# A linear-attention and FFN kernel on one core: pairs 5 and 6 turned back by a float32 product that takes the mean off, and the last pair scaled in two steps on ScalarE

## The chip, the cores and the metric

The kernel runs on one core of one Trainium2 chip. The metric is the device time of one execution in microseconds (us), the median over several runs. Engine names are those of the profile: PE (TensorE matmul), DVE (VectorE), ACT (ScalarE), POOL (GpSimd), SP (SyncE, which here only issues DMAs).

## The reference, cut to what matters

The input has 16 sequences of 256 tokens with 128 features, in float32. Twelve layers of attention without a softmax come first; then a layer norm, a gated FFN with integer weights, and a second layer norm. Only the end concerns the change:

```python
x = layernorm(x + attn(x))             # no weight, no bias; eps 1e-5
gate, up = x @ wg.T, x @ wu.T          # weights = int / 127, 384 hidden
h = silu(gate) * up
x = layernorm(x + h @ wd.T)            # (x - mean) / sqrt(var + eps), over 128 features
```

## The kernel before

The 16 sequences are worked on as 8 pairs (0 to 7) of 512 tokens each. A planner (`Plan.run`) puts the order of all instructions together when the program is built: every step is an `op` with a cost in ns for each engine that may do it, the values it reads and writes, and a due time (`prio`). The planner always emits, of the steps that could start first, the one that is due first, and gives it to the engine on which it would end first. So a changed cost or a changed list of engines for one step can move others. Each engine then works through its own list in order, and waits for other engines with semaphores.

The function `ffn(p, prio)` emits all of the work of a pair after the attention. In it, with the lines of the profile:

- `mm_r` (L675, L677) makes the tokens' rows of the residual sum in PSUM. `norm(pr, True)` is the first layer norm; its input already has zero mean ("centred").
- `tr_x` (L683) turns the result so that features lie on partitions. L205 or L207 takes a rounded high part `xh` (tile `yhl`), L686 the low part `xl` (tile `thl`), L691 or L693 the whole (tile `kv`).
- For each of three blocks of 128 hidden features: gate and up products (L706 and L707 on high and low part, 128x512 each), a Silu on ACT (L709), its product with up on DVE (L710, tiles `xt` and `qgv`), a rounded copy `hh` (L205 on ACT, L207 on DVE), the rest `hl` (L210, on POOL or DVE), and the down products (L719, L720). The third block of pair 7 goes without the split: L723, a float32 product straight from the tile that L710 wrote.
- L732 (DVE) adds the residual to the down products in PSUM, still with features on partitions. `tr_o` (L736) turns four blocks of 128 tokens back on PE. For pair 7 both are cut in two halves with a PSUM bank each.
- `norm(po, False, po2)` is the last layer norm: `stats` (L618, two instructions on DVE), `var` (L621 `ve`; L623 `nm` = minus the mean), `rstd` on POOL (L634, the power -0.5 of `ve`, and L636, `nb` = `nm` times that power), and the scaling on ACT (L650, four instructions that take `nb` as bias and the power as scale). For pair 7 the first half is scaled on DVE (L648, subtracts the mean and multiplies in one), the second on ACT (L650).
- L743 stores the pair: SP issues the DMA, for the second half of pair 7 ACT does.

A centred norm needs neither L623 nor L636; ACT scales it with the power alone (L646), or DVE does the whole pair in one instruction (L641). `center` is a 128x128 float32 matrix, the identity minus 1/128, built at the start.

Of the kernel before, what the change touches and what calls it, by code (L numbers as in the profile page):

```python
# [13 lines left out]
AF = mybir.ActivationFunctionType  # L14
ALU = mybir.AluOpType
# [6 lines left out]
C = 128  # L22
# [4 lines left out]
NP = B // PB  # L27
# [7 lines left out]
N = PB * T  # L35
K = N // 128
G = 4
NO = NP // G
OB = G * PB
WARM = 30  # L40


# [31 lines left out]
PE, ACT, DVE, POOL, SP = "pe", "act", "dve", "pool", "sp"  # L74
# [92 lines left out]
def mm32(n=C):  # L167
    return max(220, 4 * n / 2.4 + 8)
# [6 lines left out]
def act(n, sbuf=False, pointers=0):  # L175
    return (94 if sbuf else 51) + 93 * pointers + n / 1.2


def dve(n, fast=False):
    return 69 + n / (1.92 if fast else 0.96)  # L180
# [6 lines left out]
def flat(t):  # L187
    return t.rearrange("p a b -> p (a b)")
# [3 lines left out]
def linear_attention_ffn_kernel(ctx: ExitStack, tc: tile.TileContext, x, xt, wall, wq0, bias, wg, wu, wd, out):  # L192
    nc = tc.nc
# [7 lines left out]
    bank = lambda v: banks[v.slot]  # L201
# [10 lines left out]
    def mul(e, dst, a, b):  # L212
        (nc.vector if e == DVE else nc.gpsimd).tensor_tensor(dst, a, b, ALU.mult)  # L213
# [8 lines left out]
    for t in xtoks:  # L222
        nc.vector.memset(t[:, :, C:], 1.0)
    for _ in range(WARM):
        nc.tensor.matmul(banks[7][:, :128], zero, zero, start=True, stop=True)
    tst = new("tst", [B, W])
    nc.gpsimd.memset(tst[:, :, C:], 0.0)
    ident = new("ident", [128])
# [5 lines left out]
    center, centerr = new("center", [128]), new("centerr", [128], F32R)  # L234
# [136 lines left out]
    def offset_products(l, o):  # L371

        raw, pc = wts[l][0], Val("bank")
        c = tst[:, o * OB : (o + 1) * OB, C]

        def mm():
            for s in range(1 if l else 0, 3):
                for g in range(G):
                    cols = slice(32 * g, 32 * g + 32)
                    nc.tensor.matmul(bank(pc)[cols, s * OB : (s + 1) * OB], wraw[raw.slot][:, s * C : (s + 1) * C][:, cols], c, start=True, stop=True)  # L380
        return [raw, *vc[o * G : (o + 1) * G]], pc, mm

    def offsets(l, o, prio, pc):


        bs, ps = slice(o * OB, (o + 1) * OB), slice(o * G, (o + 1) * G)
        c = tst[:, bs, C]
        step = lambda costs, f, reads, writes: plan.op(costs, f, reads, writes, prio)
        src = lambda s: bank(pc)[:, s * OB : (s + 1) * OB]
        step({DVE: 133}, lambda e: nc.vector.tensor_scalar(vb[:, bs], src(2), bcol[:, l, 2:3], None, ALU.add), [pc, vbias], [vvc[o]])  # L390
# [3 lines left out]
        step({DVE: dve(32 * OB)}, lambda e: nc.vector.transpose(flat(vbb[:, bs]), vb[:, bs].unsqueeze(2).to_broadcast([128, OB, 32])), [vvc[o]], [vvb[o]])  # L394
        step({DVE: dve(32 * OB)}, lambda e: mul(e, kvo[:, bs], vbb[:, bs], kb[:, bs].unsqueeze(2).to_broadcast([128, OB, 32])), [vvb[o], vkb[o]], [vkvo[o]])

# [182 lines left out]
    for p in range(NP):  # L579
        t = {f"{n}{j}": new(f"{n}{j}_{p}", [512], F32R) for n in ("hh", "hl") for j in range(NB)}  # L580
# [14 lines left out]
    def ffn(p, prio):  # L595

        x = xts[p]
        t = lambda n: ctxs[p][n]
        bs = slice(p * PB, (p + 1) * PB)
        chunks = lambda a: a.rearrange("p (k c) -> p k c", c=C)  # L600
        v = {n: Val() for n in ("tt", "st", "rs", "x1", "xh", "xl", "sg0", "sg1", "hh0", "hh1", "hl0", "hl1")}

        def op(costs, emit, reads, writes):
            plan.op(costs, emit, reads, writes, prio)

        def norm(src, centred, other=None):


            xs, rows = t("x1"), lambda: bank(src)
            cut = lambda a, k: a[:, k * C : (k + 1) * C]  # L610
            row = lambda k: cut(bank(other if other and k >= K // 2 else src), k)

            def stats(e, ks=range(0, K, 2)):

                for k in ks:
                    b = bank(other if other and k else src)
                    both = b[:, k * C : (k + 2) * C].rearrange("p (k c) -> p c k", c=C)
                    nc.vector.bn_stats(t("st")[:, k : k + 2, :].rearrange("p k s -> p (k s)"), both)  # L618

            def var(e):  # L620
                nc.vector.tensor_scalar(t("ve"), t("st")[:, :, 2], 1.0 / C, EPS, ALU.mult, ALU.add)  # L621
                if not centred:
                    nc.vector.tensor_scalar(t("nm"), t("st")[:, :, 1], -1.0, None, ALU.mult)  # L623
            some, tiny = dve(2 * C) + 40, 75 * (2 - centred)
            if other:
                parts = [Val(), Val()]
                for k, b in ((0, src), (2, other)):
                    op({DVE: some}, lambda e, k=k: stats(e, [k]), [b], [parts[k // 2]])
                op({DVE: tiny}, var, parts, [v["st"]])
            else:  # L630
                op({DVE: K // 2 * some + tiny}, lambda e: (stats(e), var(e)), [src], [v["st"]])

            def rstd(e):
                nc.gpsimd.tensor_tensor(t("rs"), t("ve"), mhalf, ALU.pow)  # L634
                if not centred:
                    nc.gpsimd.tensor_tensor(t("nb"), t("nm"), t("rs"), ALU.mult)  # L636
            op({POOL: 1060 + 220 * (not centred)}, rstd, [v["st"]], [v["rs"]])

            def scale(e, ks=range(K)):
                if centred and e == DVE:  # L640
                    nc.vector.tensor_tensor(chunks(xs), chunks(rows()), t("rs").unsqueeze(2).to_broadcast([128, K, C]), ALU.mult)  # L641
                    return
                for k in ks:
                    d, r, rs = cut(xs, k), row(k), t("rs")[:, k : k + 1]
                    if centred:
                        nc.scalar.activation(d, r, AF.Copy, scale=rs)  # L646
                    elif e == DVE:
                        nc.vector.tensor_scalar(d, r, t("st")[:, k, 1:2], rs, ALU.subtract, ALU.mult)  # L648
                    else:
                        nc.scalar.activation(d, r, AF.Identity, bias=t("nb")[:, k : k + 1], scale=rs)  # L650
            if centred:
                costs = {DVE: dve(N), ACT: K * act(C, False, 1)}
            else:
                costs = {ACT: K * act(C, False, 2)}
            if not other:
                op(costs, scale, [src, v["rs"], v["st"]], [v["x1"]])
                return [v["x1"]]

            ends = [Val(), Val()]
            op({DVE: 2 * 319}, lambda e: scale(e, range(2)), [src, v["rs"], v["st"], v["x1"]], [ends[0]])  # L660
            op({ACT: 2 * act(C, False, 2)}, lambda e: scale(e, range(2, K)), [other, v["rs"], v["st"], v["x1"]], [ends[1]])
            return ends


        ptt, pr, px = (Val("bank") for _ in range(3))
# [6 lines left out]
        def mm_r(e):  # L672
            rows = cqs[p // G].unsqueeze(1).to_broadcast([128, 2, C])
            for b in range(PB):
                nc.tensor.matmul(bank(pr)[:, 2 * b * C : 2 * (b + 1) * C], pick[:, p % G * PB + b, :], rows, start=True, stop=False)  # L675
                for k in (2 * b, 2 * b + 1):
                    nc.tensor.matmul(bank(pr)[:, k * C : (k + 1) * C], x[:, k * 128 : (k + 1) * 128], t("tt")[:, b * C : (b + 1) * C], start=False, stop=(k % 2 == 1))  # L677
        op({PE: K * mm32() + PB * mmr(2 * C)}, mm_r, [vx[p], v["tt"], vcq[p // G], vpick], [pr])
        norm(pr, True)

        def tr_x(e):
# [15 lines left out]
        cut = 2 if p == NP - 1 else 1  # L697
        downs = [(Val("bank"), slice(i * N // cut, (i + 1) * N // cut)) for i in range(cut)]
        outs, total = [Val("bank") for _ in range(cut)], "sg1" if cut == 2 else "sg0"
        for n in range(NH):  # L700
# [15 lines left out]
            for i, (d, cols) in enumerate(downs):  # L716
# [7 lines left out]
                m = N // len(downs)  # L724
# [5 lines left out]
        for (d, cols), o, r in zip(downs, outs, sums):  # L730
            m = N // len(downs)
            op({DVE: dve(m)}, lambda e, d=d, cols=cols: nc.vector.scalar_tensor_tensor(t(total)[:, cols], bank(d)[:, cols], QSCALE, t("x1")[:, cols], ALU.mult, ALU.add), [d, v["x1"]], [r])  # L732

            def tr_o(e, o=o, cols=cols):
                for k in range(cols.start // 128, cols.stop // 128):
                    nc.tensor.transpose(bank(o)[:, k * C : (k + 1) * C], t(total)[:, k * 128 : (k + 1) * 128], ident)  # L736
            op({PE: m // 128 * 109}, tr_o, [r], [o])
        po, po2 = outs if len(outs) == 2 else (*outs, None)
        ends = norm(po, False, po2)
        m = N // len(ends)  # L740
        for i, end in enumerate(ends):
            def store(e, r0=p * N + i * m, src=t("x1")[:, i * m : (i + 1) * m]):
# [22 lines left out]
    for p in range(NP):  # L765
        if p % G == 0:
            c_rows(p // G, L + FOFF + FSTEP * p)
        ffn(p, L + FOFF + FSTEP * p - (AHEAD if p == NP - 1 else 0))
# [32 lines left out]
```

## Time and profile before

| what | value |
| --- | --- |
| runs | 306.12, 305.32, 305.22 us; median 305.32 |
| profiled execution | 305.16 us, of which the span from first to last instruction is 303.2 us |
| mean granted TensorE clock | 0.998 |
| busy share of the span | PE 97%, DVE 75%, ACT 72%, POOL 45% |
| instructions | 12834 |

The page's busy shares are means over the whole span. The FFN of all pairs lies in about the last 60 us, and the change is in its last few; there the shares are others, and the stretches have to be asked for one by one. Matmul records overlap (their ends are modelled), so for PE the distance between two starts says more than the length of a record.

### The profile page before, as it was taken

How to read it: one execution, taken by the hardware profiler on the slowest of the kernel's cores; microseconds unless marked ns; L12 is line 12 of the kernel's file. 1: busy time of each engine (PE TensorE's matmuls, PEld its weight loads, DVE VectorE, ACT ScalarE, POOL GpSimd, SP SyncE). 2: the span in 40 equal slices, each digit the busy share in tenths (PEclk: the TensorE clock that was granted, in tenths of full speed). 3: DMA queues.
4: the chain of work that ended last, by engine and by line, in shares of the span. 5: the costliest groups of instructions: out<-in, count | busy, mean ns of one | idle time of the engine just before them, and what ended most of it. 6: DMA issues, size and time to landing. Idle time of an engine off the chain costs nothing.

```text
span 303.2 us, 12834 instructions
## 1 busy us (share of the span) xinstructions
PE 294.3 (97%) x5376; PEld 269.8 (89%) x5376; DVE 226.1 (75%) x683; ACT 217.7 (72%) x559; POOL 137.8 (45%) x208
## 2 busy tenths in 40 slices
PE   8999999999999999999999999999999999999981
PEld 8989999999999999999999999989999998878760
DVE  4796887777677676876767777786644789999993
ACT  3556877867777768777686666777887558788875
POOL 8256452334531445225432354224431167777883
PEclk9999999999999999999999999999999999999999
DMA  7624213112031120311302102120000000000225
GB/s 214 163 91 131 67 39 89 38 46 82 3 89 37 39 89 4 88 40 28 98 2 56 37 17 50 49 68 17 2 2 4 3 1 2 0 0 8 63 70 138
DMA packets 22489, 15.65 MB, mean 52 GB/s; under 512 B 1952, under 2 KB 19872, under 8 KB 22432
## 3 DMA queue, kind: packets, MB, share of 16 engines
q1 hardware_dynamic: 21872, 14.62, 17.3%
q8 instruction: 42, 0.69, 0.9%
q10 hardware_dynamic: 560, 0.22, 0.3%
q14 instruction: 15, 0.12, 0.1%
HBM read 8.02 MB, written 2.10 MB: 33 GB/s over the span
## 4 chain that ended last, share of the span: by engine, by line
PE 87%; DVE 10%; issue 1%; ACT 1%; POOLq 0%; POOL 0%; DVEq 0%
PE bank L455 14%; PE bank L434 8%; PE bank L517 8%; PE bank L436 7%; PE bank L435 7%; PE bank L442 5%; PE bank L499 5%; PE bank L536 4%; PE bank L534 4%; PE bank L535 4%; PE bank L443 3%; PE bank L444 3%; PE bank L336 3%; DVE st L618 2%; PE bank L706 2%; PE bank L707 2%
## 5 line engine op out<-in xcount | busy, mean ns | idle before, releaser
L210 POOL TENSOR_TENSOR thl<-tst,thl 128x260 fp32r<-128x260 f32 x88 | 64.8, 768 | 123.1 <-ACT thl L205 123.1
L205 ACT COPY qgv<-bank 128x256 f32<-128x256 f32 x169 | 59.8, 378 | 19.2 <-PE bank L444 12.9
L205 ACT COPY kv<-bank 128x512 f32<-128x512 f32 (+1 forms) x93 | 53.4, 575 | 19.5 <-PE bank L436 14.2
L434 PE MATMUL bank<-whl,thl 128*128 128x256 f32 x176 | 51.9, 295 | 0.0
L436 PE MATMUL bank<-whl,thl 128*128 128x256 f32 x176 | 49.7, 282 | 0.0
L435 PE MATMUL bank<-whl,thl 128*128 128x256 f32 x176 | 49.4, 281 | 0.0
L455 PE MATMUL bank<-kv,g 128*128 128x128 f32 x352 | 46.1, 275 | 0.0
L541 DVE TENSOR_TENSOR tst<-bank,tst 128x260 f32<-128x260 f32 x96 | 36.9, 425 | 9.4 <-PE bank L536 9.0
L205 ACT CAST thl<-tst 128x260 fp32r<-128x260 f32 x88 | 33.0, 408 | 14.6 <-DVE tst L541 14.5
L455 PEld LDWEIGHTS bank<-kv,g 128*128 128x128 f32 x352 | 42.7, 191 | 0.4 <-issue 0.4
L448 DVE TENSOR_SCALAR qgv<-bank,bcol 128x2 f32<-128x2 f32 x88 | 19.2, 221 | 28.3 <-ACT qgv L205 22.9
L434 PEld LDWEIGHTS bank<-whl,thl 128*128 128x128 f32 x176 | 33.1, 188 | 4.0 <-issue 3.8
L530 DVE TENSOR_TENSOR yhl<-bank,yhl 128x260 fp32r<-128x260 f32 x96 | 34.4, 420 | 2.2 <-ACT yhl L205 2.1
L436 PEld LDWEIGHTS bank<-whl,thl 128*128 128x128 f32 x176 | 33.1, 188 | 0.3 <-POOL thl L210 0.2
L435 PEld LDWEIGHTS bank<-whl,thl 128*128 128x128 f32 x176 | 33.2, 189 | 0.0
L442 PE MATMUL bank<-thl,whl 128*128 128x260 f32 x88 | 28.8, 327 | 0.0
L205 ACT CAST yhl<-bank 128x260 fp32r<-128x260 f32 (+1 forms) x61 | 21.8, 408 | 8.3 <-PE bank L517 7.7
L207 DVE CAST yhl<-bank 128x260 fp32r<-128x260 f32 (+1 forms) x43 | 16.7, 430 | 12.7 <-PE bank L517 12.7
L517 PE MATMUL bank<-qgv,gm 32*32 32x130 f32 x1536 | 25.8, 280 | 0.2 <-DVE gm L213 0.2
L443 PE MATMUL bank<-thl,whl 128*128 128x260 f32 x88 | 24.8, 282 | 0.0
L444 PE MATMUL bank<-thl,whl 128*128 128x260 f32 x88 | 24.7, 281 | 0.0
L517 PEld LDWEIGHTS bank<-qgv,gm 32*32 32x32 f32 x1536 | 17.2, 103 | 5.5 <-ACT kv L205 0.3
(157 smaller groups left out, 694.7 us busy)
## 6 DMA issues: line engine op xcount, KB each, us to landing
wraw<-wall SPq DMA_DIRECT2D x12, 256.0 KB, 3.0
wpt<-whl SPq DMA_DIRECT2D x24, 96.0 KB, 2.2
qgv<-x SPq DMA_DIRECT2D x8, 256.0 KB, 5.0
xt<-xt SPq DMA_DIRECT2D x8, 256.0 KB, 3.1
out<-kv SPq DMA_DIRECT2D x7, 256.0 KB, 2.3
wpt<-whl SPq DMA_DIRECT2D x24, 64.0 KB, 2.7
wpt<-whl SPq DMA_DIRECT2D x24, 32.0 KB, 1.9
wraw<-wg SPq DMA_DIRECT2D x1, 192.0 KB, 3.2
```

What stands on the lines that cost most here:

```text
L205: nc.scalar.copy(dst, src)
L210: (nc.vector if e == DVE else nc.gpsimd).tensor_tensor(dst, a, b, ALU.subtract)
L434: nc.tensor.matmul(o, hi[:, b, 0:C], hl(0, 1, 2), start=True, stop=False)
L435: nc.tensor.matmul(o, hi[:, b, 0:C], hl(1, 1, 2), start=False, stop=False)
L436: nc.tensor.matmul(o, lo[:, b, 0:C], hl(0, 1, 2), start=False, stop=True)
L442: nc.tensor.matmul(o, hl(0, 0), flat(hi), start=True, stop=False)
L443: nc.tensor.matmul(o, hl(0, 0), flat(lo), start=False, stop=False)
L444: nc.tensor.matmul(o, hl(1, 0), flat(hi), start=False, stop=True)
L455: nc.tensor.matmul(bank(pgv)[:, b * C : (b + 1) * C], g0[p][:, b, :], tv(b), start=True, stop=True)
L517: nc.tensor.matmul(bank(pys[r])[group(g + r), b * W : (b + 1) * W], gm[group(g), r * PB + b, :], qss[p][group(g), b, :], start=True, stop= ...
L530: plan.op({DVE: dve(PB * W)}, lambda e: nc.vector.tensor_tensor(yl, bank(py)[:, : PB * W], yh.bitcast(F32), ALU.subtract), [py, vyh[p]], [ ...
L541: plan.op({DVE: dve(PB * W)}, lambda e: nc.vector.tensor_tensor(ts, bank(pw)[:, : PB * W], ts, ALU.add), [pw], [vt[p], vc[p]], prio)
```

## The change

In `norm`, "centred" now also holds for the last norm of pairs 5 and 6 (`LESS`). Their sums are turned back not by a transpose against `ident` but by a float32 product with `center` as the moving operand, which turns the block and takes the mean over the features off in the same step. L623 and L636 fall away for these two pairs; pair 5's scaling may go to DVE or ACT with the power alone, pair 6's only to DVE. Pair 7's `nm` becomes a step of its own, its `nb` goes, and the second half is scaled in two steps on ACT: the mean off, PSUM to SBUF, as soon as `nm` is there, and the multiplication by the power afterwards, in place in SBUF.

```diff
+LESS = range(5, 7)
...
             def var(e):
                 nc.vector.tensor_scalar(t("ve"), t("st")[:, :, 2], 1.0 / C, EPS, ALU.mult, ALU.add)
-                if not centred:
-                    nc.vector.tensor_scalar(t("nm"), t("st")[:, :, 1], -1.0, None, ALU.mult)
+                if not centred and not other:
+                    less()
+
+            def less():
+                nc.vector.tensor_scalar(t("nm"), t("st")[:, :, 1], -1.0, None, ALU.mult)
...
                 op({DVE: tiny}, var, parts, [v["st"]])
+                op({DVE: tiny}, lambda e: less(), parts, [vless])
...
                 nc.gpsimd.tensor_tensor(t("rs"), t("ve"), mhalf, ALU.pow)
-                if not centred:
+                if not centred and not other:
                     nc.gpsimd.tensor_tensor(t("nb"), t("nm"), t("rs"), ALU.mult)
...
             if centred:
-                costs = {DVE: dve(N), ACT: K * act(C, False, 1)}
+                costs = {DVE: dve(N), ACT: K * act(C, False, 1)} if p < NP - 2 or src == pr else {DVE: dve(N)}
...
+            def means_off(e):
+                for k in range(2, K):
+                    nc.scalar.activation(cut(xs, k), row(k), AF.Identity, bias=t("nm")[:, k : k + 1])
+
+            def scale_off(e):
+                for k in range(2, K):
+                    nc.scalar.activation(cut(xs, k), cut(xs, k), AF.Copy, scale=t("rs")[:, k : k + 1])
+            op({ACT: 2 * act(C, False, 1)}, means_off, [other, vless, v["x1"]], [vcent])
             op({DVE: 2 * 319}, lambda e: scale(e, range(2)), [src, v["rs"], v["st"], v["x1"]], [ends[0]])
-            op({ACT: 2 * act(C, False, 2)}, lambda e: scale(e, range(2, K)), [other, v["rs"], v["st"], v["x1"]], [ends[1]])
+            op({ACT: 2 * act(C, True, 1)}, scale_off, [v["rs"], vcent], [ends[1]])
...
-                    nc.tensor.transpose(bank(o)[:, k * C : (k + 1) * C], t(total)[:, k * 128 : (k + 1) * 128], ident)
-            op({PE: m // 128 * 109}, tr_o, [r], [o])
+                    turned, whole = bank(o)[:, k * C : (k + 1) * C], t(total)[:, k * 128 : (k + 1) * 128]
+                    if p in LESS:
+                        nc.tensor.matmul(turned, whole, center, start=True, stop=True)
+                    else:
+                        nc.tensor.transpose(turned, whole, ident)
+            op({PE: m // 128 * (mm32() if p in LESS else 109)}, tr_o, [r], [o])
...
-        ends = norm(po, False, po2)
+        ends = norm(po, p in LESS, po2)
```

The planner's lists for the FFN change with it, in the built program from the first gate products on. By their contents: DVE gets three more L210 subtractions (POOL three fewer), one `hh` cast fewer, no L207 copies of `tt` in this stage (two before); POOL makes three more of the L693 sums (ACT three fewer L691 copies). At the end, PE's list before is: pair 5's turn, the eight 128x256 products of pair 7, pair 6's turn, the two L723 products, pair 7's turn. After, pair 5's turn stands among the eight products, and pair 6's behind the L723 products, just ahead of pair 7's. DVE's list after the third L710 of pair 7 is then: pair 6's L732, pair 5's statistics, pair 7's two L732, pair 6's statistics, pair 7's statistics, pair 6's scaling, pair 7's first half.

More of the change, by code (lines that the diff above doesn't have):

```diff
@@ L621, in var @@
                 nc.vector.tensor_scalar(t("ve"), t("st")[:, :, 2], 1.0 / C, EPS, ALU.mult, ALU.add)
-                if not centred:
-                    nc.vector.tensor_scalar(t("nm"), t("st")[:, :, 1], -1.0, None, ALU.mult)
-            some, tiny = dve(2 * C) + 40, 75 * (2 - centred)
+                if not centred and not other:
+                    less()
+            def less():
+                nc.vector.tensor_scalar(t("nm"), t("st")[:, :, 1], -1.0, None, ALU.mult)
+            some, tiny = dve(2 * C) + 40, 75 * (2 - bool(centred or other))
+            vless = Val()
             if other:
@@ L634, in rstd @@
                 nc.gpsimd.tensor_tensor(t("rs"), t("ve"), mhalf, ALU.pow)
-                if not centred:
+                if not centred and not other:
                     nc.gpsimd.tensor_tensor(t("nb"), t("nm"), t("rs"), ALU.mult)
-            op({POOL: 1060 + 220 * (not centred)}, rstd, [v["st"]], [v["rs"]])
+            op({POOL: 1060 + 220 * (not centred and not other)}, rstd, [v["st"]], [v["rs"]])
             def scale(e, ks=range(K)):
@@ L657, in norm @@
                 return [v["x1"]]
-            ends = [Val(), Val()]
+            ends, vcent = [Val(), Val()], Val()
+            def means_off(e):
[5 more added lines that the diff above has]
+            op({ACT: 2 * act(C, False, 1)}, means_off, [other, vless, v["x1"]], [vcent])
             op({DVE: 2 * 319}, lambda e: scale(e, range(2)), [src, v["rs"], v["st"], v["x1"]], [ends[0]])
-            op({ACT: 2 * act(C, False, 2)}, lambda e: scale(e, range(2, K)), [other, v["rs"], v["st"], v["x1"]], [ends[1]])
+            op({ACT: 2 * act(C, True, 1)}, scale_off, [v["rs"], vcent], [ends[1]])
             return ends
```

## The prediction

> **What bounds the kernel now.** I read from coarse to fine. First, busy time by stretches of the FFN (length, then busy us and instructions of PE, PEld, DVE, ACT, POOL, then clock, DMA share, GB/s):
>
> ```profile
> 270.00:275.00 5.00, 5.00 (x26) 4.07 (x25) 4.93 (x10) 3.89 (x8) 3.69 (x3) 1.00 0.00 0
> 285.00:290.00 5.00, 5.00 (x28) 4.11 (x26) 4.90 (x14) 4.77 (x12) 4.46 (x6) 1.00 0.28 80
> 290.00:295.00 5.00, 4.26 (x26) 3.14 (x24) 4.93 (x14) 3.41 (x10) 4.38 (x6) 1.00 0.28 78
> 295.00:300.00 5.00, 1.84 (x8) 1.08 (x8) 3.44 (x13) 4.46 (x13) 3.12 (x6) 1.00 0.43 116
> ```
>
> PE and DVE are both full until 290, then DVE alone. The page's 75% for DVE hides this. Second, the chain that ended last (start, us, what):
>
> ```profile
> 242.97 0.45 PE bank L677 x4
> ...
> 273.78 0.44 PE bank L736 x4
> ...
> 294.50 0.59 DVE xt L710
> 295.09 0.68 DVE st L618 x2
> 295.95 0.43 DVE qgv L732
> 296.52 0.42 PE bank L736 x2
> 296.97 0.77 DVE st L618 x2
> ```
>
> From pair 7's last L710 on, the end is one serial chain. (L677 and L736 price the new product below.) Third, the timeline (start, us, engine, line, tiles):
>
> ```profile
> 260.77 1.28 POOL L693 TENSOR_TENSOR kv<-yhl,thl 128x512 f32<-128x512 f32 x1
> 260.80 1.80 DVE L210 TENSOR_TENSOR hl<-xt,hh 128x512 fp32r<-128x512 f32 x1
> 280.33 1.30 POOL L210 TENSOR_TENSOR hl<-xt,hh 128x512 fp32r<-128x512 f32 x1 [1.27 <-ACT hh L205]
> 280.72 0.94 DVE L621 TENSOR_SCALAR ve<-st 128x4 f32<-128x4 f32 x1
> 298.02 1.01 POOL L634 TENSOR_TENSOR rs<-ve,mhalf 128x4 f32<-128x4 f32 x1 [0.69 <-DVE nm L623]
> 299.06 0.73 DVE L648 TENSOR_SCALAR kv<-bank,st,rs 128x128 f32<-128x128 f32 x2 [1.05 <-POOL rs L634]
> 299.33 0.81 ACT L650 ACTIVATE kv<-bank,nb,rs 128x128 f32<-128x128 f32 x2 [0.47 <-POOL nb L636]
> ```
>
> Two things are to be seen. After the power (ends 299.03) DVE needs until 299.79, ACT, which waits for `nb` first, until 300.14; ACT's store is the last. And a DVE step that reads SBUF alone stretches beside a POOL step: 1.80 against the usual 0.69, and 0.94 against 0.17. Fourth, the DMA rates from 280 us on, in 40 slices of 0.58 us:
>
> ```profile
> GB/s 140 288 24 0 0 0 0 0 0 0 20 290 142 0 0 0 164 279 9 0 0 0 0 0 260 192 14 0 16 289 148 136 287 29 234 276 289 106 0 0
> ```
>
> The last four busy slices (299.7 to 302.0) carry pair 6 and both halves of pair 7 at nearly the 290 GB/s that no slice exceeds.
>
> **The frame.** The profiled execution took 305.16 us: 303.2 of span and 1.96 around it. It lies 0.16 below the median 305.32, so I work out a shift of the end and apply it to the median. About 0.3%, 0.92 us, is what a measurement of this kernel can tell from no change: faster means below 304.40, slower above 306.24.
>
> **Step 1: when pair 7's last L710 starts (before: 294.41).** Two engines can set it.
>
> PE: from the first gate product at 250.69, before, until the first L723: 138 products of 512 columns at 0.2325, 13 turns at 0.44, 8 products of 256 at 0.12, 6 and 6 of the residual at 0.11 and 0.445. That is 42.10, so 292.79. After: two turns fewer (pair 6's now stands behind), pair 5's product more. The chain shows two float32 products of 128 columns in 0.45, so four take 0.89, against 0.44 for four transposes: 42.11. PE's due time is unchanged; the stalls of before (0.9 by 290.93, where the third up product of pair 7 starts instead of at 290.02) may come or go: 292.8 to 293.7 for L723.
>
> DVE: from 249.01 (L686 of pair 0) to that L710, starts one behind the other: 51 steps of 0.60, 10 statistics of 0.79, 16 tiny ones of 0.08, 4 casts of 0.46 behind their source, 3 of 0.34: 42.64, so 291.65. The trace says 294.41: 2.76 were lost to stretched steps and waits. After: 52, 9, 14, 1 and 3 of these, 40.91, so 289.92 without losses. Pair 6's sum and pair 5's statistics went behind L710, one norm scaling to ACT, two copies and a cast away; three subtractions came from POOL.
>
> The losses have to be guessed. The eight subtractions of before lost 1.1 in all (the one of 1.80), 0.14 each; the tiny steps 1.25 over 16, 0.08 each. Three subtractions more and two tiny steps fewer give 2.76 + 0.42 - 0.16 = 3.0. The bounds: nothing more than before's second half lost (about 1), or three full POOL steps of 1.3 more (6.6). I take 3.0, nearest to the measured total: L710 at 292.94. L723 follows 0.73 behind, as before (294.41 to 295.14): 293.67, and PE is there by then.
>
> The GPSIMD Engine Reference of the Trainium skill (section Specifications) says that GpSimd shares its SBUF interfaces with VectorE, with contention for instructions with two SBUF inputs or in a two-port mode. That speaks against this change: the three L210 that move to DVE have two SBUF inputs. By that rule alone each could cost a whole POOL step; the rows say that one in eight did.
>
> **Step 2: from L710 to the powers.** On DVE: pair 6's sum from 293.54, pair 5's statistics from 294.14, `ve` 294.93, pair 7's two sums 295.01 and 295.35, free at 295.69. On PE: two L723 take 0.86 (four records 0.217 apart), then pair 6's product, 294.53 to 295.42; its 0.45 more than transposes hide behind DVE's sums. Without that cover it would cost 0.45. Pair 6's statistics start at 295.69, `ve` at 296.48; pair 7's statistics at 296.58 (its turns, done by about 296.3, wait for nobody), `ve` at 297.38. POOL: a power begins 0.25 behind `ve` (297.77 to 298.02) and takes 1.01, the next one 1.06 later. Pair 6's: 296.73 to 297.74. Pair 7's is ready at 297.63 but queued behind it: 297.79 to 298.80, against 299.03 before. Shift: -0.23.
>
> **Step 3: behind the power.** Two `nm`, three `nb` go; 0.16 of DVE and 0.8 of POOL, of which only the last `nb` (0.27 with its gap) was on the path. Of ACT's last two steps, 0.81 for two with bias and scale (0.36 from start to start), the mean part moves ahead. The rest reads SBUF with one pointer, a form the trace lacks. Bounds: L646, one pointer from PSUM, 2.19 for eight, 0.27 each; L650 0.36. I take 0.30, since the ACT copies of 512 columns cost 0.52 from SBUF and 0.47 from PSUM: 0.70 for two. ACT then ends at 298.80 + 0.05 + 0.70 = 299.55, against 300.14: -0.59. The added wait (mean off for `nm`, about 297.75) has only the scaling and the store queued behind it; ahead of it ACT scales pair 5 (power about 295.2 to 296.2, four of 0.27, done by 297.4), so it is free in time. DVE scales pair 6 (0.68) from 297.77 in its wait for the power; that pair's store leaves about 298.5 instead of 298.9 when ACT finished its twelve. Pair 7's first half: 299.57 against 299.79, -0.22.
>
> **Sum.** The stores now leave together, 0.59 and 0.22 earlier, and share the queue: at best the end moves with ACT, -0.59; at worst the second half waits for the first (128 KB at 289 GB/s, 0.45): -0.14. I take the middle, -0.4: span 302.8, and 305.32 - 0.4 = **304.9**. Its own range is 304.2 to 305.7.
>
> **Rivals.**
> - **Faster: PE's due time decides.** DVE loses at most 2.3, as its trace up to 280 (1.9 lost) allows; L723 then starts at 292.8 to 293.2, 0.5 to 0.9 earlier than in my sum: **304.2**. For it: L710 stands 1.73 earlier in DVE's work. Against: late tiny steps lost 0.9 in the second half.
> - **Slower: the subtractions wait for POOL.** Place: the three L210 that came to DVE. Two waits of 1.3 instead of 0.14 bring the loss to 5.3 and L723 to 296.0, +1.9: **307.2**; one gives 306.1. It decides from a loss of 3.4 (no gain); slower by over 0.3% is from 4.35. Against: DVE does them when POOL has three fewer. For: POOL instead does three L693 more.
> - **The store hides it.** If pair 6's 256 KB leave no earlier, the last slices stay full and ACT's shorter end only queues: **305.2**.
>
> **How the numbers follow.** Forecast 0.40, PE decides 0.27, waits for POOL 0.21, store hides it 0.12. Faster: 0.27 and 0.05 of the forecast's lower edge, 0.32. Slower: 0.21 and 0.02 of its upper, 0.23. The rest, 0.45, is within 0.3%. The range reaches from 303.9 (L723 at its earliest, ACT's whole 0.59) to 306.8, between one wait and two; about 0.2 lies outside.
>
> **What would show it.** Right: pair 7's last L710 at 292.5 to 293.3; pair 6's product in 0.9; two powers back to back, the second ending near 298.8; ACT's last two steps in 0.7. Wrong: L210 rows on DVE above 1.2; L723 waiting for anything but L710; the first power later than the second's `ve`; or a last store that lands no earlier although ACT is done 0.6 sooner. A new stall of PE before 290 would break step 1.

## The result, and the profile after

| | runs | median, us | profiled execution: time, span |
| --- | --- | --- | --- |
| before, same chip | 6 | 305.41 (305.08 to 306.12) | 305.16, 303.2 (the one shown above) |
| after | 6 | 307.62 (306.97 to 308.42) | 307.73, 305.6 |

After stands to before as 1.0062, with a 95% interval of 1.0045 to 1.0078: slower by some 1.9 us. The forecast was 304.9 with a range of 303.9 to 306.8, so the time lies outside, on the side of the rival "the subtractions wait for POOL".

In the changed kernel the line numbers are higher: L210 is L211, L205 is L206, L621 is L622, L618 is L619, L634 and L636 are L640 and L642, L650 is L656, L686 is L701, L693 is L708, L709 and L710 are L724 and L725, L732 is L747. In the experiments they are some ten higher again; the tiles keep their names.

Busy time by stretches of the changed kernel, same columns as before the prediction:

```profile
270.00:275.00 5.00, 5.00 (x26) 4.10 (x25) 4.97 (x8) 4.53 (x9) 3.89 (x3) 1.00 0.00 0
285.00:290.00 5.00, 5.00 (x25) 4.06 (x25) 4.96 (x12) 4.58 (x12) 3.85 (x5) 1.00 0.18 52
290.00:295.00 5.00, 4.50 (x23) 3.35 (x21) 4.75 (x12) 4.00 (x10) 4.82 (x6) 1.00 0.19 54
295.00:300.00 5.00, 3.92 (x29) 3.51 (x28) 4.87 (x13) 3.09 (x10) 2.23 (x4) 1.00 0.38 105
```

DVE is as full as before, but in the first stretch with 8 instructions and not 10: the same busy time holds less work. PE has 29 instructions in 295 to 300 where it had 8: its work ends later. The chain that ended last, after 288:

```profile
289.18 1.45 POOL hl L211 x2
290.63 1.06 issue
291.69 1.01 POOL rs L640
292.70 0.04 issue
292.78 0.21 POOL nb L642
...
293.38 1.15 ACT kv L656 x3
294.52 0.52 ACT hh L206
295.06 0.03 DVE hl L211
295.10 0.57 issue
295.67 0.68 DVE xt L725
```

Before, this part of the chain was PE and DVE. Now it runs through POOL (two subtractions, then a power queued behind them), ACT (a pair's scaling that waits for `nb`, and behind it in the same list the copy `hh`) and DVE. The timeline (start, us, engine, line, tiles) shows what became of the short steps, and the end:

```profile
252.64 1.28 POOL L708 TENSOR_TENSOR kv<-yhl,thl 128x512 f32<-128x512 f32 x1 [0.38 <-DVE thl L701]
253.19 0.75 DVE L622 TENSOR_SCALAR ve<-st 128x4 f32<-128x4 f32 x1
265.84 1.18 DVE L211 TENSOR_TENSOR hl<-qgv,hh 128x512 fp32r<-128x512 f32 x1
273.48 1.30 POOL L211 TENSOR_TENSOR hl<-xt,hh 128x512 fp32r<-128x512 f32 x1 [0.20 <-ACT hh L206]
273.75 1.30 DVE L208 CAST hh<-qgv 128x512 fp32r<-128x512 f32 x1
285.52 1.29 POOL L708 TENSOR_TENSOR kv<-yhl,thl 128x512 f32<-128x512 f32 x1
286.14 0.70 DVE L622 TENSOR_SCALAR ve<-st 128x4 f32<-128x4 f32 x1
295.06 0.69 DVE L211 TENSOR_TENSOR hl<-qgv,hh 128x512 fp32r<-128x512 f32 x1 [0.15 <-ACT hh L206]
299.51 1.98 POOL L640 TENSOR_TENSOR rs<-ve,mhalf 128x4 f32<-128x4 f32 x2 [0.60 <-DVE ve L622]
300.13 0.17 DVE L622 TENSOR_SCALAR ve<-st 128x4 f32<-128x4 f32 x1
301.53 0.73 DVE L654 TENSOR_SCALAR kv<-bank,st,rs 128x128 f32<-128x128 f32 x2 [0.29 <-POOL rs L640]
301.53 0.69 ACT L673 ACTIVATE kv<-kv,rs 128x128 f32<-128x128 f32 x2 [0.44 <-POOL rs L640]
```

A `ve` of 4 columns, 0.17 us when nothing is in its way, ends when POOL's sum ends: 252.64 + 1.28 = 253.92 against 253.19 + 0.75 = 253.94. The two powers at the end do run back to back, and beside the first of them a `ve` takes its 0.17 us.

That difference holds in all fifteen profiles, from 240 us on. All 39 `ve` and `nm` steps that began while a POOL step of 512 columns had more than 0.3 us to go ended 0.02 to 0.03 us behind it; all 20 that began so beside a power took 0.16 or 0.17. The casts and subtractions that read SBUF alone went the same way: 34 of 34 stretched beside a step of 512 columns, none of 31 beside a power. Steps that read PSUM were not stretched beside either (0.69 us at most).

Two distances sum the comparison up. The **body** is from the first low part (L686 or L701 of pair 0) to the start of pair 7's last gate-up product (L710 or L725), the **tail** from there to the end of the span. The start itself lay between 248.7 and 250.8 us in the profiled executions, though the instructions ahead of it are the same, so single spans are not compared. Body and tail are of the one profiled execution of each kernel; the ratio is of all runs.

| kernel | body, us | tail, us | ratio to before, 95% |
| --- | --- | --- | --- |
| before | 45.40 | 8.8 | 1 |
| forecast for after | 43.93 | 9.9 | 0.9986 |
| after | 45.66 | 9.9 | 1.0062 (1.0045 to 1.0078) |
| after_again | 45.66 | 9.9 | 1.0061 (1.0039 to 1.0082) |
| new_order | 45.65 | 10.9 | 1.0083 (1.0060 to 1.0105) |
| old_order | 45.32 | 8.9 | 0.9996 (0.9981 to 1.0010) |
| old_order_seven | 45.41 | 8.8 | 0.9991 (0.9976 to 1.0007) |
| whole_act | 45.41 | 9.9 | 1.0051 (1.0031 to 1.0071) |
| sums_short | 44.50 | 9.9 | 1.0017 (1.0004 to 1.0031) |
| engines_back | 49.37 | 10.4 | 1.0179 (1.0159 to 1.0199) |
| ve_pool_new | 47.37 | 11.3 | 1.0142 (1.0120 to 1.0164) |
| ve_pool_old | 45.01 | 9.0 | 0.9990 (0.9977 to 1.0003) |
| no_small_new | 44.00 | 9.7 | 0.9983 (0.9972 to 0.9995) |
| no_small_old | 43.84 | 9.0 | 0.9939 (0.9924 to 0.9953) |
| new_both | 43.73 | 9.8 | 0.9969 (0.9953 to 0.9986) |
| first_plain | 44.88 | 8.8 | 0.9983 (0.9967 to 0.9998) |

The tail came as forecast. The body should have become 1.5 us shorter and became 0.26 longer. Body and tail together are 1.4 us longer than before's.

### The profile page after: what moved, and what is told of

Same layout as the page of the kernel before. It is cut to its first block, busy times and chain, and to the rows that moved or that the text cites. A ratio compares the mean times of both kernels' runs of the same rounds, so it can differ in the third digit from the quotient of the medians.

```text
span 305.6 us, 12848 instructions
## 1 busy us (share of the span) xinstructions
PE 296.1 (97%) x5384; PEld 271.4 (89%) x5384; DVE 228.7 (75%) x681; ACT 217.4 (71%) x561; POOL 137.6 (45%) x205
## 4 chain that ended last, share of the span: by engine, by line
PE 88%; DVE 6%; ACT 2%; issue 1%; POOL 1%; POOLq 0%; DVEq 0%
PE bank L456 14%; PE bank L435 8%; PE bank L518 8%; PE bank L437 7%; PE bank L436 7%; PE bank L443 5%; PE bank L500 5%; PE bank L537 4%; PE bank L535 4%; PE bank L536 4%; PE bank L444 3%; PE bank L445 3%; PE bank L337 3%; PE bank L721 2%; PE bank L722 2%; PE bank L381 2%
## 5 line engine op out<-in xcount | busy, mean ns | idle before, releaser
L211 POOL TENSOR_TENSOR thl<-tst,thl 128x260 fp32r<-128x260 f32 x88 | 64.9, 770 | 123.5 <-ACT thl L206 123.5
L206 ACT COPY qgv<-bank 128x256 f32<-128x256 f32 x171 | 60.4, 379 | 19.0 <-PE bank L445 12.8
L206 ACT COPY kv<-bank 128x512 f32<-128x512 f32 (+1 forms) x93 | 53.4, 576 | 19.8 <-PE bank L437 14.4
L206 ACT CAST thl<-tst 128x260 fp32r<-128x260 f32 x88 | 33.0, 408 | 14.5 <-DVE tst L542 14.4
L206 ACT CAST yhl<-bank 128x260 fp32r<-128x260 f32 (+1 forms) x61 | 21.8, 405 | 7.9 <-PE bank L518 7.7
```

The costliest lines, as they stand in the source:

```text
L206: nc.scalar.copy(dst, src)
```

## The experiments

All but after_again use one means: the planner's result (step, engine, buffers) is written down as a list and replayed, so that contents and order can be exchanged. The list holds the whole kernel; its first difference between before and after lies behind the start of the FFN.

```diff
     def run(self):
-        (search for the step that could start first and is due first)
+        for step in STEPS.split(";"):
+            n, e, *slots = step.split()
+            ...
+            self.ops[int(n)].emit(e)
```

### Contents or order

Theory A: the planner's rearranged lists cost the time. Theory B: the contents (float32 product, one-pointer scaling, stores that leave together) do. Theory C: it is the FFN's start, which differs by chance.

old_order, the changed contents on the list of before:

```diff
-STEPS = (list of the changed kernel)
+STEPS = (list of before; pair 6's scaling moved to DVE, behind pair 7's mean part)
```

> The changed kernel's contents (products with center for pairs 5 and 6, pair 6 scaled on DVE, pair 7 in two steps on ACT) on the list of steps of the kernel before; only pair 6's scaling and the new mean-off step stand in new places. Theory A (the rearranged lists cost the time, through DVE steps that wait for POOL): like before or a little faster, 304.9 to 305.4, with pair 7's last L710 within 0.3 of before's 294.41. Theory B (the contents cost it: products, serial powers, pair 6 ahead of pair 7): 306.5 to 307.6. Theory C (neither: the first 250 us, which took 1.0 more in the profile after though their lists are the same): 306.0 to 306.5, with that 1.0 here too.

new_order, the contents of before on the changed list:

```diff
-LESS = range(5, 7)
+LESS = ()                 # and pair 7 with nb, in one step, as before
 STEPS = (list of the changed kernel)
```

> The contents of the kernel before (transposes, mean off by nb, pair 7 in one step on ACT) on the list of steps of the changed kernel; pair 6's scaling is on ACT as before. Theory A: 307.5 to 308.4, since pair 6's scaling on ACT now also stands just ahead of pair 7's. Theory B: 305.3 to 306.2. Theory C: 306.0 to 306.5.

after_again, the changed kernel once more, beside these:

> The changed kernel once more, beside the other three on one chip. The first 250 us have the same lists as before: if the 1.0 of the profile after is chance (of it 0.5 in the first 10 us, where the clock was granted at 6.0 us instead of 4.9), it will differ here by some tenths; if it belongs to the program, it comes back at 1.0. Median 307.2 to 308.0.

Measured: old_order 305.49 us (before, on the same chip: 305.55), new_order 307.72, after_again 307.19. The contents alone change nothing that can be measured, the list alone costs 2.2 us. So B and C fall, and of theory A it stands that the lists cost the time; whether through waits for POOL, the next runs ask. On the new list the contents even gain: the tail is 10.9 us with the contents of before and 9.9 with the changed ones. With the contents of before, POOL makes an `nb` behind each of the last three powers, and pair 6's scaling stands on ACT ahead of pair 7's: ACT is done 1.28 us behind the last power (301.01 to 302.29), in the changed kernel 0.73.

### The three sums that moved to POOL

whole_act gives the L708 sums of pairs 1, 3 and 7 back to ACT, as copies:

```diff
-1642 pool   1716 pool   1871 pool
+1642 act    1716 act    1871 act
```

> The changed kernel with the three sums of a pair's high and low parts that had moved from ACT to POOL (pairs 1, 3 and 7) given back to ACT, as copies of 0.47, at the same places of the list. If those POOL steps cost 0.5 each on DVE (the ve steps at 253.19, 259.06 and 286.14 of the profile after took 0.75, 0.67 and 0.70 against 0.17), the three ve rows fall to 0.2 and the time to 306.0 to 306.5. If the three subtractions that went to DVE are the cost, or the contents: 307.3 to 307.9.

Measured: 306.88 us, some 0.3 below after_again, which the intervals do not tell from no change, and between the two expectations. The three stretched `ve` are gone, but ACT's list is longer by three copies, and now DVE waits for ACT: in the body DVE stands idle for 1.1 us, in the changed kernel for 0.2. Timeline of whole_act:

```profile
252.38 0.17 DVE L633 TENSOR_SCALAR ve<-st 128x4 f32<-128x4 f32 x1
259.15 0.69 DVE L736 SCALAR_TENSOR_TENSOR qgv<-bank,qgv 128x512 f32<-128x512 f32 x1 [0.64 <-ACT qgv L735]
286.36 0.69 DVE L222 TENSOR_TENSOR hl<-qgv,hh 128x512 fp32r<-128x512 f32 x1 [0.38 <-ACT hh L217]
```

So this didn't price the sums. sums_short does: it makes them small and puts nothing elsewhere, so it leaves out the rest of these sums.

```diff
+                some = slice(0, 4 if p in (1, 3, 7) else N)
-                nc.gpsimd.tensor_tensor(t("x1"), t("xh").bitcast(F32), t("xl").bitcast(F32), ALU.add)
+                nc.gpsimd.tensor_tensor(t("x1")[:, some], t("xh").bitcast(F32)[:, some], t("xl").bitcast(F32)[:, some], ALU.add)
```

> The changed kernel with the three whole sums that moved to POOL (pairs 1, 3 and 7) cut from 512 columns to 4, so the rest of these residuals is missing; nothing is put on ACT in their place. If the moved sums are the price of the re-plan (three waits of DVE of 0.5 to 0.6 us, and 3 x 1.2 us of POOL ahead of powers and subtractions), the time falls by 1.2 to 2 us to 305.6 to 306.4. If the order of the other steps is the price, it stays within 0.5 of 307.4 us.

Measured: 306.18 us, ratio 1.0017 against 1.0062: 0.45% or 1.4 us less, as the first theory had it. The body falls by 1.16, the tail stays. In the rows of its body the small steps of DVE lose 1.09 us to stretching instead of 2.65. The run also takes some 3.2 us of work off POOL's list, so it prices the three sums as a whole and does not part DVE's waits from an earlier POOL.

### Engines without the order

engines_back keeps the new order of steps and gives 22 of them the engine that they had before:

```diff
-(whole sums 1642, 1716, 1871: pool; hl 1648, 1655, 1803, 1810, 1885: dve; 1625, 1854: pool; ...)
+(whole sums: act; these hl: pool; those two: dve; ...)
```

> The changed kernel's step order, kept as it is, but every step that the planner had given to another engine than before goes back to the engine it had (three whole sums to ACT, seven subtractions between DVE and POOL, six rounded copies, a few smaller ones; 22 steps in all), except pair 6's last scaling, which stays on DVE. If the wrong engines are the cost (three sums more on POOL beside DVE's steps, three subtractions more on DVE), the time comes back to 305.4 to 306.0 us. If the order is the cost, it stays at 307.0 to 307.8. In between, near 306.5, the two share it.

Measured: 311.13 us, worse than either theory allowed; the question was put wrongly. The planner's choice of engines belongs to its order: with the old engines the new order puts `nb` so late that ACT, which works in order, stands for 3.1 us at one scaling. Waits of engines_back (what waited, for what: us in total, times, longest):

```profile
POOL hl L222 <- ACT hh L217: 5.4, 7, 2.0
ACT hh L217 <- DVE xt L736: 5.1, 5, 1.5
...
ACT kv L667 <- POOL nb L653: 3.1, 1, 3.1
```

### The small steps off DVE

ve_pool_new and ve_pool_old move `ve` and `nm` to POOL, just ahead of the power, on the new and on the old list, for every norm but the last one of pair 7 (the expectations here and below say "pairs 0 to 6", but pair 7's first norm is changed too):

```diff
             def var(e):
-                nc.vector.tensor_scalar(t("ve"), t("st")[:, :, 2], 1.0 / C, EPS, ALU.mult, ALU.add)
-                if not centred and not other:
-                    less()
+                if other:
+                    nc.vector.tensor_scalar(t("ve"), t("st")[:, :, 2], 1.0 / C, EPS, ALU.mult, ALU.add)
...
             def rstd(e):
+                if not other:
+                    nc.gpsimd.tensor_scalar(t("ve"), t("st")[:, :, 2], 1.0 / C, EPS, ALU.mult, ALU.add)
+                if not centred and not other:
+                    nc.gpsimd.tensor_scalar(t("nm"), t("st")[:, :, 1], -1.0, 0.0, ALU.mult, ALU.add)
                 nc.gpsimd.tensor_tensor(t("rs"), t("ve"), mhalf, ALU.pow)
```

> The changed kernel, same order and engines, but for pairs 0 to 6 the small steps ve and nm (128x4) are done by POOL just ahead of its power, and not by DVE. If DVE's steps that wait for POOL's long SBUF steps are the term that was mis-sized (in the changed kernel's profile six ve rows of 0.39 to 0.75 us instead of 0.17 lost some 2.7 us together), pair 7's last product of gate and up starts 1 to 3 us earlier after the start of the FFN than the 45.66 of the changed kernel, and the time falls to 305.0 to 306.5 us. If the chain over ACT (its in-order waits for nb, four of 0.3 to 0.5 us, then hh, then hl) sets that product, the longer POOL step (0.2 to 0.4 more) gains nothing: 307.2 to 308.0. Another way to come to nothing: the subtractions of DVE take over the waits that ve had.

> The changed contents on the step order of before, and ve and nm of pairs 0 to 6 on POOL. With the waits of ve for POOL gone (some 1.3 us over the stage) the wait of 0.8 us ahead of the two float32 down products of pair 7 shrinks; at most that is to be had, since PE is due there anyway: 304.7 to 305.2 us by the theory of the waits, 305.5 by the theory that they are covered elsewhere, up to 306 if POOL's longer chain delays ACT's scalings.

Measured: ve_pool_new 310.25 us, 2.4 above the changed kernel's ratio (1.0142 against 1.0062); ve_pool_old 305.37, no difference to before. On the new list two things come together. POOL's chain to `nb` gets longer by 0.4 us per norm that has a mean part, or by up to 0.9 where POOL now waits for DVE, and DVE stands idle for 4.0 us in the body. And the subtractions on DVE take over the waits that `ve` had, as the expectation said they might: they lose 3.1 us instead of 0.6. ve_pool_new:

```profile
257.74 1.29 POOL L722 TENSOR_TENSOR kv<-yhl,thl 128x512 f32<-128x512 f32 x1
257.76 1.81 DVE L222 TENSOR_TENSOR hl<-xt,hh 128x512 fp32r<-128x512 f32 x1
...
286.85 0.69 DVE L222 TENSOR_TENSOR hl<-qgv,hh 128x512 fp32r<-128x512 f32 x1 [0.17 <-ACT hh L217]
286.88 0.72 POOL L651 TENSOR_SCALAR ve<-st 128x4 f32<-128x4 f32 x1
...
295.96 0.20 POOL L651 TENSOR_SCALAR ve<-st 128x4 f32<-128x4 f32 x1
```

The first `ve` stands beside the DVE subtraction (286.85 to 287.54) and ends 0.06 us behind it; the second beside none.

### The small steps left out

no_small_new and no_small_old leave `ve` and `nm` of the same norms out, without a replacement, on the two lists:

```diff
             def var(e):
-                nc.vector.tensor_scalar(t("ve"), t("st")[:, :, 2], 1.0 / C, EPS, ALU.mult, ALU.add)
-                if not centred and not other:
-                    less()
+                if other:
+                    nc.vector.tensor_scalar(t("ve"), t("st")[:, :, 2], 1.0 / C, EPS, ALU.mult, ALU.add)
...
-                nc.gpsimd.tensor_tensor(t("rs"), t("ve"), mhalf, ALU.pow)
+                nc.gpsimd.tensor_tensor(t("rs"), t("ve") if other else t("st")[:, :, 2], mhalf, ALU.pow)
                 if not centred and not other:
-                    nc.gpsimd.tensor_tensor(t("nb"), t("nm"), t("rs"), ALU.mult)
+                    nc.gpsimd.tensor_tensor(t("nb"), t("st")[:, :, 1], t("rs"), ALU.mult)
```

> The changed kernel with the small DVE steps of the norms of pairs 0 to 6 left out: no ve and no nm, the power and nb are taken straight from the statistics, so 1/128, eps and the sign of the mean part are missing. POOL's and ACT's lists stay as they are. 20 steps of 0.08 us (1.6) go, and with them nearly all of the waits of such steps for POOL (some 2.9 us in the changed kernel's profile). If DVE's own list with these waits sets pair 7's last product of gate and up, it comes 2 to 4 us earlier after the start of the FFN than 45.66, down to where PE is due, and the time is 304.5 to 306.2 us. If the chain over ACT and POOL sets it, it gains under 0.5: 307.0 to 307.7.

> The same work left out of the changed contents on the step order of before. Here PE waits only 0.8 us for pair 7's last product, so at most that and what the small steps take behind it: 304.5 to 305.2 us. Beside the same on the new order this tells whether the two orders differ by more than DVE's waits: if both come to the same time within 0.5, the waits are the whole difference; if the new order is still 1 us or more behind, it is the order of the transfers between ACT, POOL and DVE as well.

Measured: 305.01 us on the new list (0.79% or 2.4 us below the changed kernel), 303.82 on the old one (0.57% or 1.7 us below old_order, and below the range expected). These steps thus help to set the last product in both, by much, but not alone: of DVE's work and waits ahead of it some 3.8 us were taken away on the new list (14 steps of 0.08, and 2.65 of waits), and the product came only 1.66 earlier. Since `ve` also stands ahead of POOL's power, the runs do not part DVE's own list from the chain over POOL and ACT that begins at `ve`. DVE and ACT of no_small_new, from its timeline:

```profile
293.75 0.69 DVE L222 TENSOR_TENSOR hl<-qgv,hh 128x512 fp32r<-128x512 f32 x1 [1.36 <-ACT hh L217]
```
```profile
291.71 1.50 ACT L666 ACTIVATE kv<-bank,nb,rs 128x128 f32<-128x128 f32 x4 [1.54 <-POOL nb L652]
293.10 0.63 ACT L217 CAST hh<-qgv 128x512 fp32r<-128x512 f32 x1
```

With these steps out of the way, ACT's list is the next limit: a scaling waits 1.54 us for POOL, `hh` stands behind it, DVE behind `hh`.

new_both leaves out both the small steps and the three sums, on the new list:

```diff
+                some = slice(0, 4 if p in (1, 3, 7) else N)       # as in sums_short
...
-                nc.vector.tensor_scalar(t("ve"), ...)             # as in no_small_new
```

> The changed kernel with both pieces of work left out: the small DVE steps of pairs 0 to 6, and all but 4 columns of the three whole sums that moved to POOL. On the step order of before the same small steps left out gave 303.8 us. If the moved sums and DVE's waits are the whole difference of the two orders, 303.6 to 304.2 us. If something else in the new order costs as well (the later scalings on ACT, the longer tail of DVE behind the last product), 304.4 to 305.0.

Measured: 304.68 us, ratio 0.9969 against no_small_old's 0.9939: 0.9 us behind it, so the first theory is out. The bodies are now alike (43.73 and 43.84); what is left is the tail (9.8 and 9.0). DVE stands idle in them for 2.7 and 1.8 us, so its own list no longer sets the body alone; what does, no run here shows. The new list pays some 0.8 to 1.1 us in the tail in any case.

### Pair 7's two steps alone

old_order_seven is the kernel before with this one part of the change:

```diff
-                nc.scalar.activation(cut(xs, k), row(k), AF.Identity, bias=t("nb")[:, k : k + 1], scale=t("rs")[:, k : k + 1])
+                nc.scalar.activation(cut(xs, k), row(k), AF.Identity, bias=t("nm")[:, k : k + 1])
...
+                nc.scalar.activation(cut(xs, k), cut(xs, k), AF.Copy, scale=t("rs")[:, k : k + 1])
```

> The kernel before with one part of the change alone: pair 7's nm as a step of its own, no nb, and ACT's two steps for the second half. By the sum of the prediction for the steps behind the power ACT is done some 0.6 us earlier, so 304.7 to 305.0 us; if the two last stores, which then leave together, take back what ACT gains, 305.2 to 305.5.

Measured: 305.54 us, ratio 0.9991 (0.9976 to 1.0007): no gain. Timeline of old_order_seven:

```profile
298.68 1.01 POOL L651 TENSOR_TENSOR rs<-ve,mhalf 128x4 f32<-128x4 f32 x1 [0.69 <-DVE nm L638]
299.41 0.64 ACT L680 ACTIVATE kv<-bank,nm 128x128 f32<-128x128 f32 x2
299.91 0.71 ACT L684 ACTIVATE kv<-kv,rs 128x128 f32<-128x128 f32 x2
```

The mean part starts late, since pair 6's scaling (on ACT here) stands ahead of it until 299.4; so ACT is done 0.93 us behind the power (299.69 to 300.62), where before it was 1.11 (299.03 to 300.14). The last transfer then takes 2.1 us from issue to landing instead of 1.9, and from the power's end to the end of the span it is 4.2 us in both.

### The first norm's `ve` left out of the kernel before

The old list showed the same sensitivity to DVE's small steps, so the first norm's `ve` was taken away, with its eps, on the kernel before:

```diff
-                nc.vector.tensor_scalar(t("ve"), t("st")[:, :, 2], 1.0 / C, EPS, ALU.mult, ALU.add)
+                if src is not pr:
+                    nc.vector.tensor_scalar(t("ve"), t("st")[:, :, 2], 1.0 / C, EPS / C, ALU.mult, ALU.add)
...
-                nc.gpsimd.tensor_tensor(t("rs"), t("ve"), mhalf, ALU.pow)
+                nc.gpsimd.tensor_tensor(t("rs"), t("st")[:, :, 2] if src is pr else t("ve"), mhalf, ALU.pow)
...
-... AF.Silu, scale=QSCALE)          ... bank(o), QSCALE, t(sg) ...         ... bank(d)[:, cols], QSCALE, t("x1") ...
+... AF.Silu, scale=QSCALE * C ** 0.5)   ... bank(o), QSCALE * C ** 0.5, t(sg) ...   ... bank(d)[:, cols], QSCALE / C ** 0.5, t("x1") ...
```

> The kernel before, with its own step order, but ve of the first norm left out in all eight pairs: the power is taken straight from the sum of squares, the missing factor (the root of 128) goes into the constants of Silu, of the product with up and of the sum, and the last norm's eps is divided by 128. Only the first norm's eps of 1e-5 is missing. On DVE 7 steps of 0.08 us go ahead of pair 7's last product, and one wait for POOL of 0.3 us with them, 0.9 us in all, against the 0.8 us that PE waits for that product. If DVE's list sets the product in the order of before too, 304.6 to 305.1 us, which would be faster than both kernels; if ACT or POOL is next behind DVE, 305.2 to 305.5.

Measured: 304.71 us beside 305.58 for before, ratio 0.9983 (0.9967 to 0.9998). It is faster than the changed kernel, and than the kernel before by half a microsecond, of which the interval only just excludes no change; the body is 0.52 us shorter, which agrees. Four of the `ve` that are gone stood in the body, one of them stretched to 0.48.

## Why the prediction was wrong

**The step that failed is the first: when pair 7's last L710 starts.** Its term "loss", taken as 3.0 us, measured 4.75: the start of the body is 250.01, the list without losses 40.91, the product began at 295.67. The formula itself closes: 1.75 us more loss on the forecast span of 302.8, and 1.0 for the later start of the FFN in this execution, give 305.55; the span was 305.6. The forecast's own threshold (slower by over 0.3% from a loss of 4.35) was crossed. By the rows of the body, in us:

| lost by DVE | before | forecast | after |
| --- | --- | --- | --- |
| short steps (`ve`, `nm`) | 1.25 | 1.1 | 2.65 |
| subtractions | 1.1 | 1.5 | 0.6 |
| `hh` copies | 0 | 0 | 0.9 |
| idle and the rest | 0.4 | 0.4 | 0.6 |
| sum | 2.76 | 3.0 | 4.75 |

The mean loss of a short step, 0.08, was carried over from before; after the change it was 0.19. The mean of the subtractions was carried over in the same way. "One in eight" was no rate: the row of 1.80 was the only one of the eight subtractions that began with more than 0.3 us of a POOL step of 512 columns to go. So what counts is which pairs of steps meet, and a mean of the old list does not tell that.

**What was left out of the term.** The loss was priced for what DVE gained, three subtractions, and the change in POOL's list stood only as a word for the rival: "POOL instead does three L693 more". The runs price those at 1.4 us (sums_short). In the changed kernel's rows, three `ve` behind the moved sums lost 0.58, 0.50 and 0.53 us against their 0.17, three more beside POOL's subtractions 0.57, 0.31 and 0.22, and one `hh` copy that stood behind a POOL subtraction took 1.30 instead of 0.41. The subtractions that moved to DVE lost little: of all of them on DVE, one row took 0.81 and one 1.18 instead of 0.68. So the rival had the right sign and size, and the wrong victims; the sign that the prediction had named, an L210 row on DVE above 1.2 us, did not appear (1.18 at most).

The Trainium skill has the rule that fits: the page "SBUF — State Buffer", section "Who interferes with whom", says that a DVE copy, cast or tensor_scalar can enter a two-port mode and then takes the port pair that it shares with GpSimd, which whoever started first holds for its whole instruction. Beside POOL's steps of 512 columns the rows agree: a `ve` ends within 0.02 us of the POOL sum. Beside a power, which is a POOL instruction of 1.01 us, they do not: there no `ve` waited, and the measurement decides. The sentence of the GPSIMD Engine Reference that the prediction used names the two-port mode as well, but the prediction applied it to the steps with two SBUF inputs alone.

**"Two engines can set it" was wrong as well.** PE and DVE were weighed; the third way is ACT's list, in order, behind POOL's powers. The chain of the changed kernel runs through it, in no_small_new DVE waits 1.36 us for it, and in ve_pool_new, which lengthens it, the time rises by 2.4 us, though the subtractions' waits are part of that. In the changed kernel's body this chain ended last, but by little: DVE stood idle for 0.15 us ahead of the last subtraction, and for 0.2 in the whole body.

**Step 2 was right.** From that product to the end of the second power: forecast 5.86 us, measured 5.82 (295.67 to 301.49). Pair 6's float32 product ran from 297.38 to 298.30 behind DVE's sums, the powers back to back.

**Step 3 was right in its parts and wrong in its sum.** ACT's last two steps took 0.69 us, forecast 0.70, and ACT was done 0.73 us behind the power. But from the power's end to the end of the span it was 4.17 us before and 4.14 after: the outcome of the rival "the store hides it", with 0.12, came here. Both halves leave together, and the later transfer takes 2.4 us to land instead of 1.9. The DMA rates of the changed kernel, from 280 us to the end:

```profile
GB/s 0 0 0 26 258 143 8 0 0 0 79 289 42 0 0 0 70 290 50 0 0 0 13 0 218 192 0 0 96 287 26 0 29 291 178 283 226 222 0 0
```

The last two busy slices, in which both halves travel, carry 226 and 222; before, 276 and 289 were followed by one of 106. The reason that the rival gave, full slices, is not in these rates: the last two are below the 290 of a full one. That leaving together is what makes the later half land late is likely from the runs (2.3 to 2.4 us in after, after_again and old_order, where the two left less than 0.1 us apart), but what holds it is not shown.

**What stays open.** Corrected for the loss, the forecast moves to 304.9 + 1.75 = 306.65 us; the runs' medians are 307.2 and 307.6. Some 0.5 to 1 us is not accounted for, and body and tail together explain 1.4 of the measured 1.9 us against before. The rest is of the size by which the FFN's start differs between executions, and the profiled execution of before had one of the early starts (249.01).

## What to carry to other kernels

When a planner orders the steps, price its whole new list, engine by engine, and not the edit: the edit was worth nothing here, the new list cost 2 us. Work moved onto GpSimd had a second price here, on VectorE: a short scalar step, cast or subtraction that read SBUF alone stood until GpSimd's step of 512 columns ended, though not beside a power. So count such pairs in the list. And of an end that is made earlier, ask first whether the last stores can leave earlier without meeting each other.

## What was not expected of the hardware

A 128x4 step on DVE waits for the whole rest of a POOL step of 512 columns: 0.17 us alone, 0.67 to 0.75 beside a POOL sum of 1.28. Beside a power of 128x4, which takes POOL 1.01 us, it does not wait: 0.16 or 0.17 in 20 of 20 rows. The wait goes both ways: POOL's `ve` took 0.20 us alone and 0.72 beside a DVE subtraction, and one POOL sum 1.75 instead of 1.28. Two stores of 128 KB that left less than 0.1 us apart landed after 2.0 and 2.4 us; 0.35 us apart, in the kernel before, they took 1.9 each.
